# Layer 0 with all seven outer products split into seven unit products, third sums kept in place, and new orders

## The chip, the cores and the metric

The kernel runs on one core of one Trainium2 chip. The metric is the device time of one execution in microseconds (us). TensorE (PE in profiles) multiplies; its weight loads are shown apart as PEld. VectorE is DVE, ScalarE is ACT, GpSimd is POOL, and SyncE (SP) issues nearly all transfers. TensorE's results go to PSUM, eight banks of 512 float32 columns on 128 partitions. GpSimd does not read PSUM in this kernel: VectorE and ScalarE take results out.

## The reference

There are 64 graphs ("batches" b) of 256 nodes with 512 features. Everything is float32.

```python
def layer0(x, adj, W):                       # W: 512 x 1024
    deg = jnp.sum(adj, axis=-1, keepdims=True)
    agg = jnp.einsum('bij,bjf->bif', adj, x) / jnp.maximum(deg, 1e-6)
    out = jnp.einsum('bnf,of->bno', jnp.concatenate([x, agg], axis=2), W)
    return jax.nn.relu(out)
x = layernorm(x + layer0(x, adj, W))

def layer1(x, adj, Wq, Wk, Wv, Wo):          # biases left out here
    q, k, v = heads(x @ Wq.T), heads(x @ Wk.T), heads(x @ Wv.T)   # 8 heads of 64
    s = (q @ k.T) * 64 ** -0.5 * (adj + adj)
    return (softmax(s) @ v) @ Wo.T
x = layernorm(x + layer1(x, adj, ...))
```

## The kernel before, in words

**Layer 0 is reordered.** The kernel first multiplies x by both halves of W (for the node itself, m = 0, and for the neighbours, m = 1), and then multiplies the neighbour half, called y, by adj. The tile `oy[b % 2]` holds both results: index m, token half t (rows 0 to 127 or 128 to 255) and output half n (256 columns each).

**Seven products for eight.** Every large product is cut into 2 x 2 blocks and made of seven products and some sums and differences (the Winograd form of Strassen's method). The left sums are called 1 to 4 (`chain_sums`): S1 = A21 + A22, S2 = S1 - A11, S3 = A11 - A21, S4 = A12 - S2. The products are numbered 1 to 7; product 5 uses S1, 6 uses S2, 7 uses S3, 3 uses S4; 1, 2 and 4 use the blocks themselves. Block A21 stands in sums 1 and 3 only. The results are added as they are taken out of PSUM.

**Two levels in layer 0.** For a pair of batches (b even, and b + 1), the outer product k of layer 0 is a product of a 2 x 2 grid (batch of the pair by chunk of 128 features) with a 2 x 2 grid (chunk by m). `split_product(k)` makes it of seven unit products, each one matmul of 128 x 128 with 128 x 256 (line 546): left sums `Ls{k}1` to `Ls{k}4` on GpSimd (line 567), unit products `L{k}{q}` on TensorE, `Le{k}{q}` to take them out (lines 557 on ScalarE, 559 on VectorE). In the kernel before this is done for k in `SPLIT = (1, 5, 6, 7, 3, 4)`. Product 2 is not split: step `L2` makes two matmuls of 512 columns for each batch (line 598), and `Lj2` adds them to block (1, 0) as it stores block (0, 0) (line 603). `La12` and `La22` are sums of blocks on GpSimd (lines 607, 611). The first pair of batches (0 and 1) does not use these steps but a one-level form, steps `P1` to `P7`.

**Banks.** A PSUM bank is taken anew for each accumulator, eight in rotation. In the split products and in the product with adj, one accumulator `a` takes products 1, 6, 7 and 4, in turn and each added to the last; a second bank (`cb`) holds two accumulators, `c` (products 5 and 3) in columns 0 to 255 and `b` (product 2) in columns 256 to 511. For the product with adj these are the tiles Ya and Ycb, the steps `Y1` to `Y7` on TensorE (line 709), and `Yk*` and `Yj*` on VectorE (line 731), which scale by the degree and add. `Yk5` and `Yj3` read the half that Y5 and Y3 write; `Yj2` reads the half that Y2 writes.

**Layer 1** has steps Q, V and O in the same one-level form (lines 620, 493), scores `Sa` to `Sd` (817), their masking and maxima `ma` to `md` on VectorE (833), exponentials (`e`, `f`) and scaling (`n`) on ScalarE, a transposition through VectorE and through memory (`T`, `Dw`, `Ds`), and contexts `C0a` to `C1b` (934). `Dz*`, `Dx`, `Dadj`, `Drest`, `Dout` are transfers, `xT`, `aT`, `x1T` transpositions on VectorE, `W*` loads and sums of weights.

**The order** is written out by hand-readable lists and nothing else sets it: each engine executes its instructions in the order of the lists. `START` and `END` name steps with batches; `PLAN` is one turn for two batches, with offsets to the turn's even batch, and runs for 28 turns (`range(FIRST_TURN, B // 2 - LAST_TURNS)`, 2 to 29). A turn holds work of several batches at once: layer 0 of later ones beside layer 1 of earlier ones.

Of the kernel before, what the change touches and what calls it, by code (L numbers as in the profile page):

```python
# [10 lines left out]
ALU = mybir.AluOpType  # L11
AX = mybir.AxisListType

P = 128
# [34 lines left out]
    Dsc:0 bS2:2 Yk1:2 Y2:2 xT0:5 L37:2 bS3:2 xT0:4 Y6:2 Q4:1 bS4:2 Yk6:2 Yj2:2 aS4:2 xT1:4 Qj3:1 Y3:2
    Dza:3 Qk4:1 Y7:2 Le37:2 Yj3:2 Q2:1 Yj7:2 AYr0:2 AYb0:2 Y4:2 L34:2 xT1:5 AYp0:2 Le44:2 C1a:0 Yk4:2  # L50
    AYr1:2 bS1:3 C0a:0 AYn0:2 AYb1:2 xS3:4 C0b:0 Qj2:1 AYp1:2 C1b:0 Le34:2 aT:3 c1:0 Sc:1 bS3:3 c0:0
    Ls11:4 Sd:1 AYn1:2 mc:1 aS1:3 aS3:3 Sa:1 Dway:2 xS1:5 Dza:4 Sb:1 md:1 cS3:0 xS1:4 V2:1 ma:1 Ls51:4
    O2:0 cS1:0 Y5:3 mb:1 Y1:3 Ma:1 Ls12:4 O1:0 aS2:3 O5:0 Ok1:0 Mb:1 bS2:3 Yk1:3 Dz1:2 eb:1 L51:4 Ok5:0
    Mc:1 L15:4 Vj2:1 cS2:0 Y6:3 ec:1 Yk5:3 Y2:3 Ls53:4 Yk6:3 O6:0 Dx:3 Ls14:4 fc:1 aS4:3 Y7:3 Ok6:0
    cS4:0 fa:1 L55:4 Oj2:0 L52:4 Yj7:3 Ls52:4 O7:0 bS4:3 Le51:4 Dadj:4 fb:1 xS3:5 L56:4 Y4:3 ea:1 O3:0
    x1T:2 Y3:3 rb:1 rc:1 yS3:2 Yj3:3 nb:1 Q1:2 Yk4:3 yS1:2 Yj2:3 AYr0:3 V5:2 Qk1:2 ra:1 Oj7:0 AYr1:3
    Q5:2 na:1 AYb0:3 Tb:1 O4:0 yS2:2 Le56:4 nc:1 L12:4 AYp0:3 AYb1:3 Dwb:1 Q6:2 Ta:1 Ls54:4 AYn0:3 Md:1
    AYp1:3 Ok4:0 L57:4 Dwa:1 Qk6:2 Oj3:0 V1:2 Tc:1 AYn1:3 L11:4 Q7:2 lb1:0 Vk1:2 Dwc:1 Le11:4 Le55:4
    lb0:0 Qk5:2 Le12:4 V6:2 lp0:0 Le57:4 Qj7:2 L16:4 Vk6:2 L54:4 ed:1 Dsa:1 Q4:2 xS2:5 Le16:4 Ls13:4
    Le15:4 ln0:0 yS4:2 Dsb:1 L17:4 Le54:4 lp1:0 L53:4 Vk5:2 L13:4 L2:4 Le13:4 xS2:4 ln1:0 Ls71:4 fd:1  # L60
    Ls61:4 V3:2 Dway:3 Ls62:4 Ls64:4 rd:1 Dout:0 Q3:2 nd:1 Ls63:4 Vj3:2 Le53:4 Lj2:4 Le52:4 Qk4:2 L2:5
    Le17:4 Qj3:2 Td:1 L14:4 L61:4 Le14:4 Dwd:1 V2:2 Le61:4 Dsc:1 V7:2 L66:4 Vj7:2 Q2:2 Lj2:5 Drest:1
    Le66:4 L67:4 Qj2:2 L65:4 Dsd:1 V4:2 Le65:4 Le67:4 L62:4 Vj2:2 Vk4:2 L63:4 Le62:4 L64:4 deg:4 xS4:5
    Sa:2 aT:4 xS4:4 Sc:2 Le64:4 Dz1:3 bo:1 C0a:1 C1a:1 ma:2 Dzx:7 C0b:1 Ls31:4 Le63:4 c0:1 Ls72:4 mc:2
    C1b:1 Ls32:4 Ma:2 Ls74:4 c1:1 Dx:4 Sb:2 Ls34:4 fa:2 La12:4 Sd:2 mb:2 L75:4 cS1:1 L35:4 md:2 Ls73:4
    L71:4 Mb:2 O1:1 Mc:2 La12:5 ec:2 L32:4 Ok1:1 Dadj:5 O5:1 Le71:4 eb:2 Md:2 x1T:3 L72:4 cS2:1 O2:1
    ed:2 Le75:4 aS1:4 Le72:4 O6:1 Ls33:4 fb:2 Le35:4 cS3:1 L76:4 aS3:4 ea:2 L33:4 Le76:4 cS4:1 L73:4
    Ok6:1 L31:4 Le33:4 fd:2 Le73:4 O7:1 Le31:4 rb:2 fc:2 Ok5:1 L41:4 ra:2 Oj7:1 L77:4 Le32:4 na:2 L36:4
    Ls41:4 Le77:4 O4:1 Le36:4 rd:2 Oj2:1 bS1:4 L74:4 Ok4:1 Y1:4 rc:2 yS1:3 Ta:2 nc:2 O3:1 La22:4 Q5:3
    Le74:4 Dwa:2 Oj3:1 nb:2 Dzx:6 Ls42:4 Le41:4 yS3:3 deg:5 Y5:4 L37:4 bS2:4 nd:2 L45:4 Le37:4 V5:3  # L70
    aS2:4 Tb:2 La22:5 L46:4 L34:4 Tc:2 Dwb:2 Ls44:4 Q1:3 Dsa:2 bS3:4 Le45:4 Ls43:4 Le46:4 Yk1:4 yS2:3
    L42:4 Qk1:3 Le34:4 L47:4 Dwc:2 Y6:4 Le47:4 Vk5:3 V1:3 Td:2 aS4:4 L44:4 Vk1:3 L43:4 Le42:4 Qk5:3
    Dwd:2 Le44:4 V6:3 Dsb:2 Le43:4 Yk5:4 Q6:3 lb1:1 Yk6:4 lb0:1 Y3:4 Dsc:2 Qk6:3 yS4:3 Y7:4 Q2:3 lp1:1
    Yj7:4 Vk6:3 xT0:6 Yj3:4 bS3:5 ln1:1 xT1:6 Y2:4 bS4:4 Q7:3 xT1:7 Dsd:2 lp0:1 V7:3 ln0:1 Qj7:3 Y4:4
    Vj7:3 Dout:1 V3:3 Yk4:4 xT0:7 V2:3 Vj3:3 xS1:7 Yj2:4 Q3:3 AYr0:4 xS1:6 Dza:5 AYb0:4 Q4:3 Qj3:3
    AYr1:4 AYb1:4 V4:3 Qk4:3 Qj2:3 AYp1:4 C1a:2 Drest:2 Dza:6 C0a:2 AYp0:4 AYn1:4 C0b:2 Ls13:6 AYn0:4
    C1b:2 Ls51:6 aT:5 Vk4:3 Dway:4 c0:2 Vj2:3 aS1:5 Sa:3 c1:2 Ls11:6 Sb:3 bS1:5 ma:3 cS1:2 Sc:3 cS3:2
    Sd:3 mb:3 aS3:5 bo:2 O2:2 mc:3 Y1:5 Y5:5 Dx:5 O5:2 Yk1:5 Ma:3 md:3 aS2:5 O1:2 ea:3 Ls52:6 bS2:5 Y2:5
    Dz1:4 fa:3 L15:6 Ok1:2 Mb:3 cS2:2 Y6:5 L51:6 ra:3 Oj2:2 bS4:5 L11:6 Yk6:5 O6:2 Yk5:5 aS4:5 Le11:6
    Le51:6 Md:3 Ls53:6 Y7:5 ed:3 Ok6:2 Mc:3 Y3:5 Yj2:5 Ls12:6 L12:6 cS4:2 Yj3:5 fc:3 L56:6 Ok5:2 L16:6  # L80
    Le56:6 O7:2 AYr0:5 Le16:6 ec:3 O3:2 Yj7:5 Oj7:2 na:3 AYb0:5 Y4:5 L55:6 Yk4:5 L57:6 AYp0:5 Oj3:2 L2:6
    AYr1:5 fd:3 AYb1:5 AYn0:5 O4:2 rc:3 x1T:4 AYp1:5 nc:3 L17:6 L2:7 lb0:2 Ls54:6 yS1:4 AYn1:5 Le12:6
    Tc:3 Ls14:6 Le55:6 L52:6 Dway:5 Le15:6 eb:3 V1:4 Dadj:6 Le57:6 rd:3 L13:6 Ok4:2 fb:3 Le17:6 L54:6
    lb1:2 Q1:4 xS2:6 nd:3 Dwc:3 Le13:6 lp0:2 rb:3 Le52:6 Ta:3 L14:6 Le54:6 xS2:7 Vk1:4 V5:4 Le14:6 Qk1:4
# [70 lines left out]
def kernel(  # L155
# [36 lines left out]
    nc = tc.nc  # L192
# [5 lines left out]
    G = F // 2  # L198
# [70 lines left out]


    OUTER = {1: B11, 2: B21, 3: B22, 4: T4, 5: T1, 6: T2, 7: T3}
    SPLIT = (1, 5, 6, 7, 3, 4)
    w0_inner = const.tile([P, len(SPLIT), 3, G], F32, name="W0_inner")

    def inner_weights(k):
# [756 lines left out]
```

## Time and profile before

| | |
|---|---|
| Median of 3 runs | 3019.8 us (3018.74 to 3021.39) |
| The profiled execution | 3019.61 us, span 3017.7 us |
| TensorE clock granted, mean | 0.997 |
| Busy: TensorE, VectorE, GpSimd, ScalarE | 98%, 74%, 60%, 54% |
| Matmul records | 18700 (two for each float32 matmul) |
| Data moved by DMA | 509.69 MB, 169 GB/s |

A span is the time from the first to the last instruction of the profiled execution. In a timeline each line has the start, the length (both in us), the engine, the source line, the operation, what it writes and reads, the shapes and the number of instructions; a bracket gives the engine's idle time just before and what ended it. In the list of waits a line has who waited for whom, the sum in us, how often, and the longest. In groups of instructions the mean length of one stands behind the busy time. The records of following matmuls overlap, since they are pipelined.

### The profile page before, as it was taken

To read this page: it belongs to the slowest core of one execution; us is meant where nothing else is said; L and a number is where in the kernel's file an instruction comes from. 1 tells how busy PE (TensorE), PEld (TensorE's weight loads), DVE (VectorE), ACT (ScalarE), POOL (GpSimd) and SP (SyncE) were. 2 spreads that over 40 slices of the span, in tenths; PEclk is the share of its full clock that TensorE was granted. 3 is DMA by queue.
4 is the path that set the end of the run, shared out by engine and by line. 5 is a ranking of instruction groups with operands and counts; after the bars stand their busy time and mean duration, and the time that the engine had idled before them with its cause. 6 is when DMAs were issued, how large, how long until landed. Compare 5 with 4: busy or idle time off the path is not lost.

```text
span 3017.7 us, 59666 instructions
## 1 busy us (share of the span) xinstructions
PE 2972.0 (98%) x18700; PEld 2541.1 (84%) x18700; DVE 2219.4 (74%) x6148; ACT 1638.0 (54%) x4999; POOL 1818.5 (60%) x3315
## 2 busy tenths in 40 slices
PE   7999999999999999999999999999999999999997
PEld 4888888888888888888888888888888888888886
DVE  6877777777777777777777877777777777777774
ACT  2556556456555565554554645555556555455465
POOL 5655656656566566566556665666665656656653
PEclk9999999999999999999999999999999999999999
DMA  8476566775666666667656667666676566765663
GB/s 175 130 191 177 147 178 161 185 186 155 174 166 160 193 172 160 174 159 192 177 149 181 157 177 186 166 166 171 156 195 179 147 178 161 186 186 151 178 175 99
DMA packets 491402, 509.69 MB, mean 169 GB/s; under 512 B 113616, under 2 KB 390096, under 8 KB 491088
## 3 DMA queue, kind: packets, MB, share of 16 engines
q1 hardware_dynamic: 490768, 505.35, 64.6%
q8 instruction: 152, 2.49, 0.4%
q14 instruction: 162, 1.33, 0.2%
q10 hardware_dynamic: 320, 0.52, 0.1%
HBM read 306.45 MB, written 199.23 MB: 168 GB/s over the span
## 4 chain that ended last, share of the span: by engine, by line
PE 91%; DMA 3%; DVE 3%; POOL 2%; issue 1%; SPq 0%; ACT 0%; DVEq 0%; ACTq 0%; POOLq 0%
PE Qa L620 15%; PE pc L934 8%; PE Qc L620 8%; PE Va L493 7%; PE Oa L493 6%; PE Qb L620 4%; PE Vc L493 4%; PE L L598 4%; PE Ya L709 3%; PE Oc L493 3%; PE Ycb L709 3%; PE scd L817 2%; DMA z<-way 2%; PE L6a L546 2%; PE L4a L546 2%; PE L3a L546 2%
## 5 line engine op out<-in xcount | busy, mean ns | idle before, releaser
L636 ACT ACTIVATE qk<-Qa,bqk 128x128 f32<-128x128 f32 x768 | 217.9, 366 | 331.7 <-PE Qa L620 331.6
L432 POOL TENSOR_TENSOR xS<-xT,xS 128x256 f32<-128x256 f32 x64 | 47.1, 737 | 286.2 <-PE L6a L546 283.1
L852 ACT ACTIVATE sc<-sc,nmaxc 128x256 f32<-128x256 f32 x256 | 127.0, 498 | 157.7 <-POOL nmaxc L846 147.0
L649 ACT COPY v<-Va 128x256 f32<-128x256 f32 x192 | 73.0, 380 | 240.0 <-PE Va L493 240.0
L950 ACT COPY cT<-pc 128x512 f32<-128x512 f32 x128 | 74.7, 585 | 201.2 <-PE pc L934 197.9
L833 DVE CUSTOM_DVE_ANT_0 sa<-sca,adj 128x256 f32<-128x256 f32 x256 | 93.2, 421 | 110.2 <-PE sca L817 99.4
L852 ACT ACTIVATE sa<-sa,nmaxa 128x256 f32<-128x256 f32 x256 | 127.5, 502 | 68.8 <-DMA z<-way 38.7
L791 POOL TENSOR_TENSOR rest<-rest,bo_sb 128x512 f32<-128x512 f32 x128 | 160.4, 1275 | 0.0
L876 ACT ACTIVATE sc<-sc,totalc 128x256 f32<-128x256 f32 x252 | 107.5, 497 | 96.0 <-DVE totalc L864 96.0
L672 POOL TENSOR_TENSOR mv<-mv,neg_half 128x1 f32<-128x1 f32 x256 | 143.3, 560 | 21.3
L671 POOL TENSOR_SCALAR mv<-mv 128x1 f32<-128x1 f32 x256 | 58.4, 228 | 158.6 <-DVE mv L666 145.0
L731 DVE SCALAR_TENSOR_TENSOR oy<-Ya,deg,oy 128x256 f32<-128x256 f32 x256 | 121.5, 474 | 39.7 <-PE Ya L709 39.5
L833 DVE CUSTOM_DVE_ANT_0 sd<-scd,adj 128x256 f32<-128x256 f32 x256 | 93.1, 420 | 60.5 <-PE scd L817 60.5
L620 PEld LDWEIGHTS Qa<-yS,Wq 128*128 128x128 f32 x1024 | 124.4, 192 | 15.3 <-issue 13.4
L567 POOL TENSOR_TENSOR xs<-xS 128x128 f32<-128x128 f32 x248 | 122.6, 509 | 23.0 <-PE L1a L546 22.8
L677 ACT ACTIVATE x<-oy,mv 128x512 f32<-128x512 f32 x128 | 98.1, 811 | 69.7 <-POOL mv L673 69.7
L611 POOL TENSOR_TENSOR oy<-oy 128x512 f32<-128x512 f32 x62 | 77.9, 1274 | 93.6 <-DVE oy L559 93.4
L876 ACT ACTIVATE sd<-sd,totald 128x256 f32<-128x256 f32 x252 | 107.7, 508 | 45.7 <-DVE totald L864 45.6
L731 DVE SCALAR_TENSOR_TENSOR oy<-Ycb,deg,oy 128x256 f32<-128x256 f32 x192 | 91.4, 477 | 52.9 <-PE Ycb L709 52.7
L852 ACT ACTIVATE sb<-sb,nmaxb 128x256 f32<-128x256 f32 x256 | 126.5, 496 | 6.5 <-POOL nmaxb L846 6.5
L852 ACT ACTIVATE sd<-sd,nmaxd 128x256 f32<-128x256 f32 x256 | 126.7, 497 | 3.4 <-POOL nmaxd L846 3.4
L658 DVE TENSOR_TENSOR rest<-Oa,rest 128x256 f32<-128x256 f32 x192 | 80.3, 418 | 65.2 <-PE Oa L493 42.3
(311 smaller groups left out, 10029.2 us busy)
## 6 DMA issues: line engine op xcount, KB each, us to landing
zx<-in_x_dram SPq DMA_DIRECT2D x256, 128.0 KB, 4.7
x<-in_x_dram SPq DMA_DIRECT2D x256, 128.0 KB, 2.7
way<-x SPq DMA_DIRECT2D x64, 512.0 KB, 3.6
z<-way SPq DMA_DIRECT2D x256, 128.0 KB, 3.9
rest<-way SPq DMA_DIRECT2D x64, 512.0 KB, 4.8
out_dram<-rest SPq DMA_DIRECT2D x256, 128.0 KB, 3.2
wsd<-sd SPq DMA_DIRECT2D x63, 512.0 KB, 4.4
wsb<-sb SPq DMA_DIRECT2D x63, 512.0 KB, 3.8
```

The lines of the kernel that those rows point to most:

```text
L493: nc.tensor.matmul(ps[:, :width].rearrange("p (m o) -> p m o", o=G), lhsT=left(k, b, c), rhs=w(OUTER[k])[:, :, c], start=first and c == 0, ...
L546: nc.tensor.matmul(accumulator(q, b), lhsT=lefts[q](b), rhs=w[q], start=q in (5, 1), stop=True, skip_group_check=True)
L620: nc.tensor.matmul(ps.rearrange("p (m j q) -> p m j q", m=2, j=2)[:, m, j], lhsT=wqk(OUTER[k])[:, m, c, j * P : (j + 1) * P], rhs=left_y(k ...
L636: nc.scalar.activation(part_q(b, t, n)[:, m, j], ps.rearrange("p (m j q) -> p m j q", m=2, j=2)[:, m, j], AF.Identity, bias=bqk[:, m, c : ...
L672: nc.gpsimd.tensor_tensor(mv[:, 1:2], mv[:, 1:2], neg_half, ALU.pow)
L709: nc.tensor.matmul(ps[:, G:] if acc == "b" else ps[:, :G], lhsT=left(b), rhs=right(b), start=k in (5, 1), stop=True, skip_group_check=True,)
L731: nc.vector.scalar_tensor_tensor(h, ps[:, G:] if acc == "b" else ps[:, :G], held["deg", b][:, t : t + 1], h, ALU.mult, ALU.add)
L791: nc.gpsimd.tensor_tensor(rest, rest, bo_sb, ALU.add)
L833: nc.vector.tensor_tensor_reduce(out=s[:, :, :, r], in0=sc(b, j)[:, t].rearrange("p (a c l) -> p a c l", a=A, l=L), in1=held["adj", b][:, ...
L852: nc.scalar.activation(rows(b)[:, r], rows(b)[:, r], AF.Exp, bias=of("nmax", b)[:, r : r + 1], accum_out=of("total", b)[:, r : r + 1],)
L876: nc.scalar.activation(dst, src, AF.Identity, scale=of("total", b)[:, r : r + 1])
L934: nc.tensor.matmul(ps[j * D : (j + 1) * D, hp % 2], lhsT=held["v", b][:, c, h * D : (h + 1) * D], rhs=held[f"s{name}", b][:, :, c, j * NT ...
```

## The change

Product 2 of layer 0 joins the split ones: `SPLIT` becomes `(1, 5, 2, 6, 7, 3, 4)`, the steps `L2` and `Lj2` go, and `L21` to `L27`, `Ls21` to `Ls24`, `Le21` to `Le27` and `W0i2` come. The first results of product 2 (q in 5, 1, 6, 4) are stored with block (1, 0) added, on VectorE. The buffers of small sums alternate over all the products of all pairs. Sums 3 of the left sides `yS` and `cS`, and of y (`bS3`), are written over block A21 (for y, block (0, 1)), which no product reads, in place of a buffer of their own. The three lists are new throughout.

```diff
-    SPLIT = (1, 5, 6, 7, 3, 4)
+    SPLIT = (1, 5, 2, 6, 7, 3, 4)
...
         def place(b, n):
-            return part_of(s, b, [P, 2, 2, P])[:, n]
+            return block(b, 1, 0) if n else part_of(s, b, [P, 2, P])
...
         def unit_sum(b, n):
-            return part_of(f"xs{k}", b, [P, 4, P], tag=f"xs{SPLIT.index(k) % 2}")[:, n - 1]
+            return part_of(f"xs{k}", b, [P, 4, P], tag=f"xs{(b // 2 * len(SPLIT) + SPLIT.index(k)) % 2}")[:, n - 1]
...
-        t, n = {5: (1, 1), 3: (0, 1)}.get(k, (1, 0))
+        t, n = {5: (1, 1), 3: (0, 1), 2: (0, 0)}.get(k, (1, 0))
...
                 if k in (1, 5) and q in (5, 1, 6, 4):
                     nc.scalar.copy(dst, ps)
+                elif k == 2 and q in (5, 1, 6, 4):
+                    nc.vector.tensor_tensor(dst, ps, oy_block(b + beta, m, 1, 0), ALU.add)
                 else:
                     nc.vector.tensor_tensor(dst, ps, dst, ALU.add)
...
-    @step("L2")
-    def _(b):
-        ps = bank("L2", b).rearrange("p (m o) -> p m o", m=2)
-        for c in range(2):
-            nc.tensor.matmul(ps, lhsT=x_block(b, 0, 1)[:, c], rhs=w0(B21)[:, :, c], start=c == 0, stop=c == 1)
-
-    @step("Lj2")
-    def _(b):
-        ps = held["L2", b].rearrange("p (m o) -> p m o", m=2)
-        nc.vector.tensor_tensor(both(b, 0, 0), ps, both(b, 1, 0), ALU.add)
...
     def y_sum(k):
-        return lambda b: part_of(f"yB{int(k == 3)}", b, [P, G])
+        return y_block(0, 1) if k == 3 else lambda b: part_of("yB", b, [P, G])
```

Of the lists, here is the stretch of `PLAN` in which the product with adj of the turn's later batch (+3) stands, before and after, and the stretch after in which product 2 stands:

```diff
-    mc+1 Ls52+4 bo+0 V2+1 mb+1 O2+0 Dx+3 O5+0 ma+1 Mc+1 fc+1 Y5+3 O1+0 aS2+3 Dz1+2 cS2+0 Y1+3 Ok1+0
-    L51+4 Ls12+4 Yk5+3 Y2+3 Yk1+3 Ma+1 Le51+4 bS2+3 O6+0 ec+1 Vj2+1 Oj2+0 Md+1 L56+4 Ok6+0 ed+1 Y6+3
-    Dza+4 L15+4 Yk6+3 aS4+3 O7+0 cS4+0 rc+1 Ok5+0 nc+1 Yj2+3 Y3+3 Mb+1 xS3+4 L55+4 Yj3+3 L52+4 bS4+3
+    Ls51+4 Dz1+2 md+1 Sc+1 Ma+1 bo+0 fa+1 Y5+3 Y1+3 mb+1 ea+1 Dx+3 O2+0 O1+0 aS2+3 Yk1+3 Md+1 ra+1 mc+1
+    O5+0 bS2+3 na+1 Y2+3 cS2+0 L15+4 Dadj+4 Ok1+0 Mb+1 Y6+3 Yk5+3 fd+1 Mc+1 L12+4 cS3+0 Yk6+3 O6+0 ec+1
+    aS4+3 Ls12+4 L11+4 Ls52+4 Ok6+0 Y7+3 Ok5+0 Ls54+4 L51+4 Yj7+3 bS4+3 O7+0 Le51+4 x1T+2 Le11+4 cS4+0
+    fb+1 Y3+3 L56+4 Ls14+4 Yj3+3 Y4+3 ed+1 yS1+2 Oj7+0 L16+4 Yj2+3 O3+0 rd+1 Ta+1 nd+1 O4+0 Yk4+3 V1+2
...
+    Le13+4 V7+2 Le17+4 Dsd+1 L54+4 Qk5+2 Vj7+2 L21+4 xS2+5 L14+4 Le21+4 Ls21+4 aT+4 Le14+4 Q7+2 nb+1
+    yS4+2 xS2+4 L25+4 Ls22+4 Dsc+1 ln1+0 Ls24+4 Tb+1 V3+2 Ls23+4 V4+2 Le25+4 L53+4 Dwb+1 Vk4+2 L26+4
+    Le54+4 Ls61+4 L22+4 Le26+4 aS3+4 L23+4 Ls62+4 lb0+0 L65+4 Dsa+1 Ls63+4 L61+4 lp0+0 L62+4 Le61+4 Q3+2
```

## The prediction

> **What bounds the kernel now.** I read the page first: engine table, then chain.
>
> ```profile
> span 3017.7 us, 59666 instructions
> PE 2972.0 (98%) x18700; PEld 2541.1 (84%) x18700; DVE 2219.4 (74%) x6148; ACT 1638.0 (54%) x4999; POOL 1818.5 (60%) x3315
> ...
> PE 91%; DMA 3%; DVE 3%; POOL 2%; issue 1%; SPq 0%; ACT 0%; DVEq 0%; ACTq 0%; POOLq 0%
> ```
>
> TensorE is the bound: 98% busy and 91% of the chain that ends last; the other engines have a quarter of the span or more to spare. So only TensorE work and TensorE waits move the time. Next, the waits of TensorE:
>
> ```profile
> PE Pa L576 <- DMA zx<-in_x_dram: 10.9, 1, 10.9
> PE Ycb L709 <- DVE oy L731: 8.1, 29, 1.4
> PE Ycb L709 <- POOL nmaxb L846: 4.5, 28, 0.2
> ```
>
> Apart from the start, one tile has repeated waits: Ycb, some 29 and 28 times, so once each per turn of two batches (the list PLAN runs 28 turns). The timeline of TensorE, then of VectorE (L731), shows one turn:
>
> ```profile
> 1524.51 0.59 PE L546 MATMUL L5a<-W_sums,xS 128*128 128x256 f32 x2
> 1525.32 0.70 PE L709 MATMUL Ycb<-oy,aT 128*128 128x256 f32 x2 [0.21 <-DVE oy L731]
> 1525.86 1.03 PE L493 MATMUL Oa<-Wo_sums,cS 128*128 128x256 f32 x4
> 1526.72 0.59 PE L546 MATMUL L5a<-W_inner,xs 128*128 128x256 f32 x2
> 1527.15 0.59 PE L709 MATMUL Ya<-yB,aS 128*128 128x256 f32 x2
> 1527.58 0.59 PE L546 MATMUL L1cb<-W_inner,xs 128*128 128x256 f32 x2
> 1528.01 1.03 PE L493 MATMUL Oa<-Wo,cS 128*128 128x256 f32 x4
> 1529.20 0.67 PE L709 MATMUL Ycb<-oy,aS 128*128 128x256 f32 x2 [0.16 <-POOL nmaxb L846]
> 1529.71 0.59 PE L546 MATMUL L5cb<-W_inner,xs 128*128 128x256 f32 x2
> ```
>
> ```profile
> 1524.79 0.48 DVE L731 SCALAR_TENSOR_TENSOR oy<-Ycb,deg,oy 128x256 f32<-128x256 f32 x1
> ...
> 1528.58 0.47 DVE L731 SCALAR_TENSOR_TENSOR oy<-Ycb,deg,oy 128x256 f32<-128x256 f32 x1
> ```
>
> Read starts, not durations: records overlap (0.59 long, but the next starts 0.43 later). A step of 256 columns has a pitch of 0.43 (1526.72 to 1527.15 to 1527.58 to 1528.01), and a double one 0.86. Two steps break it. Y2 (Ycb<-oy,aT) starts 0.81 after a single step, 0.38 late; the step after Y2 starts 0.54 after it, 0.11 late. Y3 (Ycb<-oy,aS) starts 1.19 after a double step, 0.33 late, and the one after it 0.08 late. Together 0.90 us a turn. Both begin as a VectorE read of the other half of their bank ends: Yk5 reads columns 0 to 255 at 1524.79 and Y2 writes 256 to 511; Yj2 reads the upper half at 1528.58 and Y3 writes the lower. The name nmaxb is a mislabel: its step is long over.
>
> Product 2 of layer 0 on TensorE:
>
> ```profile
> 1545.00 1.88 PE L598 MATMUL L<-W,xT 128*128 128x512 f32 x4
> 1546.71 0.59 PE L546 MATMUL L1a<-W_inner,xT 128*128 128x256 f32 x2
> 1547.15 1.88 PE L598 MATMUL L<-W,xT 128*128 128x512 f32 x4
> 1548.86 1.95 PE L620 MATMUL Qa<-yS,Wq 128*128 128x128 f32 x16
> ```
>
> One batch's L2 takes 1.71 us (two matmuls of 512 columns; a matmul is two records), a pair of batches 3.42.
>
> **What the Trainium skill says.** "PSUM — Partial Sum Buffer", section "PSUM bank collisions raise a hardware error": two engines must not touch one bank at once on the same partitions, even at disjoint columns, and waits are to guard the bank, not the address. The trace agrees: Y2 and Y3 wait for a read of the half that they don't write (0.38 and 0.33 us). "Perfetto Trace Analysis", "Identifying the Most-Contended Engine": a high busy share of matmuls does not tell how near TensorE is to its limit. Agreed: 0.38 us is lost at Y2 and the bracket shows 0.21. The same page, "Matmuls", says that larger matmuls are more efficient where possible. Here not so: 1.71 for two of 512 columns is 0.43 for 256, the pitch of the small ones, so seven small for eight is a real seventh-eighths.
>
> **The change part by part.**
>
> (a) Product 2 as units. The built program has 1519 matmuls of 128x256 at the unit line where it had 1302, and none of 124 of 128x512: 31 pairs, 7 units for 4 long ones. Per pair 7 x 0.43 = 3.01 against 3.42, so -0.41; times 31: **-12.7 us**, wholly on the bounding engine. Only the first pair keeps its old form.
>
> (b) Its evictions: 7 on VectorE of 128x256 (line 559: 0.42 us) replace 2 of 128x512 (line 603: 0.67): +2.9 - 1.3 = +1.6 us per pair. Four more small sums on GpSimd at 0.46 to 0.51 (line 567): +1.9 us per pair. A turn is some 92.6 us, of which VectorE is busy 74%, GpSimd 60%; they become 76% and 62%. Cost 0, hidden under TensorE. Without that cover it is at most 1.6 x 31 = 50 us (VectorE) or 59 (GpSimd). Four weight sums (W0i2) run once on VectorE, 0.57 to 0.85 each by line 287: 2.6 us, in START between V5:0 and Qk1:0, well ahead of L21:2; 0, or +2.6 if bare.
>
> (c) Third sums written over a block that no product reads (yS3, cS3, bS3): as many GpSimd instructions (768 at line 432 before; 640 and 128 after), same sizes, 0. They free SBUF. A new ordering is that S1 must have read the block before S3 overwrites it; both are GpSimd's, in that order already. What they write is freed later than a separate tile was: x1T only when Q7 and V7 are done, but it was held for Q2 and V2 anyway, which come near the end.
>
> (d) The orders. In the old odd half of a turn Y2+3 stood straight behind Yk5+3, Y3+3 straight behind Yj2+3. In the new one Y2+3 stands ahead of Yk5+3 (O2, O1, O5, then Y2, L15, Y6, and only then Yk5), and Y3+3 ahead of both Yj3+3 and Yj2+3. So the two waits change sides: Yk5 now waits on VectorE for Y2. Behind it queue Yk6 and the Ok steps; for Yk5 waits Y3, with L12, O6, L11, Y7, L51, O7 between: 4 x 0.43 + 2 x 0.86 = 3.4 us for a step of 0.48. The even half was clear before and is after. **-0.90 x 28.5 = -25.7 us** (28 turns, and half a turn for what the 29 waits show beyond PLAN).
>
> (e) The rest of the reordering. The closest pairs of product, eviction and next product on one bank in PLAN have 1.3 us of TensorE work between them, in both orders (L51 to L56, for one); the old ones ran without a wait. In the new, Q5+1 takes the place of a bank that Le34 may free with 0.87 us (O3) between, where an eviction of 0.42 and its tail fit narrowly, and Q1 to Q6 has 2.2 us for four ScalarE copies of 0.37 each: tight. Not shown before: I bound (e) by nothing gained, -3 (parts of START), and one wait like Y2's per turn, +0.49 x 28 = +14; I take +1. SP issues as many DMAs (2953 instructions both); weight loads Wv and Wo swap places behind the first four loads, which stay, so the 10.9 us start stays. The seven TensorE gaps that I count in START between 31 and 53 us sum to 6.7 us (1.36, 0.96, 1.13, 0.85, 0.83, 0.93, 0.67) and may grow or shrink by a few; likewise the end, where the last softmax drains. Score and context steps stand together once per batch in both orders, so changes of matmul shape stay.
>
> Sum: the profiled run took 3019.6 us, span 3017.7; it equals the median (3019.8) to 0.2. 3019.6 - 12.7 - 25.7 + 1 = **2982 us**, 1.25% less.
>
> **Rivals.**
> - *Only the units pay.* The waits turn up elsewhere (the tight places of (e)): 3019.6 - 12.7 = 3007, with part of them 2992 to 3007. For: product 2 now holds two banks from L21 to L24, across 14 other TensorE steps, where L2 and Lj2 freed theirs at once. Against: the old order has, away from the halves, no repeated wait at all.
> - *The change misses its wait.* Y2's lateness comes from something else than Yk5, such as its operand; then (d) gives nothing, again near 3007. Against: the read of the other half ends 0.05 us before Y2 starts (1524.79 + 0.48) and 0.15 before Y3 (1528.58 + 0.47), the same way in two places with different operands.
> - *Slower.* Product 2 is a serial chain on VectorE: its first evictions read the result of product 1 and must come before those of product 6 add to the same block. If VectorE is behind there (after its 16 score instructions, which start 0.345 apart, 5.5 us, or a transpose of 1.2), L6 holds TensorE. Price: up to the 2.9 us of seven evictions per turn; from (12.7 + 25.7) / 28.5 = 1.35 us a turn it decides. At 2.0 it gives 3019.6 - 38.4 + 57 = 3038. Against: those 14 other steps lie among the seven, and VectorE idles 26%.
>
> **How the numbers follow.** Measurement resolves about 0.2% (6 us). Forecast 0.71, within 2973 to 2991. Units only, in whole or part, 0.20, 2991 to 3010. About nothing 0.03 (3014 to 3026), slower 0.06. A low end of 2972 takes in (e)'s gain and a START and an end better by some us; a high end of 3003 takes most of the second case. Faster 0.91, same 0.03, slower 0.06.
>
> **What would show it.** Right: TensorE rows at the unit line count 3038, none at 128x512 for layer 0; turns of 91.3 us instead of 92.6; Ycb no longer among TensorE's repeated waits; VectorE waits for Ycb instead. (a) is wrong if unit starts are over 0.45 apart; (d) if Y2 or Y3 still starts late, or another TensorE wait shows some 28 times; the whole if VectorE's L evictions release TensorE waits of over 1 us a turn.

## The result, and the profile after

The changed kernel took 2989.4 us (median of 4 runs, 2988.0 to 2989.9) against 3019.3 us for the kernel before (4 runs beside it, 3018.3 to 3021.4). The ratio is 0.9899 with a 95% interval of 0.9882 to 0.9917: 29.9 us, or 1.0%, faster. The forecast was 2982 us with 2973 to 2991 as its likeliest range, so the direction and the range held. The sum, 37.4 us, was 7.5 us too large. Where these went is the main subject of what follows.

From the page of the kernel after, the engine table and the chain that ended last:

```profile
span 2987.9 us, 60252 instructions
PE 2946.9 (99%) x18886; PEld 2578.8 (86%) x18886; DVE 2255.2 (75%) x6307; ACT 1650.5 (55%) x4999; POOL 1868.5 (63%) x3439
...
PE 96%; DMA 2%; DVE 1%; issue 1%; POOL 1%; ACT 0%; SPq 0%; ACTq 0%; POOLq 0%; DVEq 0%
```

TensorE has 186 records more than before (31 pairs, 14 records in place of 8; these are shorter) and is busy 25 us less. That is more than the shorter records give (12.6, below): part of the old waits stood in the busy time, as at Y2, which was 0.38 late with 0.21 in its bracket. Its share of the chain rose from 91% to 96%: there is less waiting left to remove.

The four longest waits of TensorE after (who waited for whom, us in total, times, longest):

```profile
PE Pa L582 <- DMA zx<-in_x_dram: 10.9, 1, 10.9
PE L2a L550 <- DVE oy L563: 3.3, 1, 3.3
PE p_bv L351 <- DMA Wo<-in_wot_dram: 3.3, 1, 3.3
PE Ya L704 <- POOL yB L573: 2.0, 1, 2.0
```

Ycb's 29 and 28 waits are gone (one of 1.4 us in START is left). Each of these four occurs once, and all lie in the prologue (START). Two are new beside the first kernel, 3.3 us each. In VectorE's list Ycb stands with

```profile
DVE oy L726 <- PE Ycb L704: 8.8, 29, 0.7
```

In the kernel before, VectorE waited for Ycb more, not less (86 times, 52.7 us), so this list alone does not show that a wait changed sides. The timeline does, for one step.

Here is TensorE in the odd half of a turn of the kernel after, and below it two lines of VectorE's:

```profile
1149.39 1.03 PE L497 MATMUL Oc<-Wo_sums,cS 128*128 128x256 f32 x4
1150.25 0.59 PE L704 MATMUL Ycb<-oy,aT 128*128 128x256 f32 x2
1150.68 0.59 PE L550 MATMUL L1cb<-W_inner,xs 128*128 128x256 f32 x2
...
1154.14 1.03 PE L497 MATMUL Oa<-Wo,cT 128*128 128x256 f32 x4
1155.00 0.60 PE L704 MATMUL Ycb<-oy,aS 128*128 128x256 f32 x2
1155.43 0.59 PE L550 MATMUL L5a<-W_inner,xs 128*128 128x256 f32 x2
```

```profile
1150.88 0.48 DVE L726 SCALAR_TENSOR_TENSOR oy<-Ycb,deg,oy 128x256 f32<-128x256 f32 x1 [0.29 <-PE Ycb L704]
...
1155.63 0.48 DVE L726 SCALAR_TENSOR_TENSOR oy<-Ycb,deg,oy 128x256 f32<-128x256 f32 x1
```

Read the starts. Y2 (Ycb<-oy,aT) starts 0.86 after a double step and Y3 (Ycb<-oy,aS) too, and the steps behind both follow after 0.43. Nothing is late. VectorE, at Yk5's read of the other half, now stands idle 0.29 us until Y2 has ended, and nothing on TensorE waits for it.

**The turn.** I measure a turn from the start of V2 of one even batch to that of the next, and take the median of the turns of one profiled run. Before it is 92.58 us, after 91.29: 1.29 less, 36.2 us over 28 turns. The forecast was 91.3.

**The whole span, divided.** Give each TensorE record the start-to-start time that its shape shows where nothing is late (0.216 us for 256 columns; two records make a step of 0.43), add these up, and call all that a record starts later than this a stall. Then the end of TensorE's work is its first start plus the pitches plus the stalls. START stands for stalls ahead of 190 us, the tail for those in the last 30 us of TensorE's work. All from one profiled run each:

| us | pitches | stalls in START | between | tail | TensorE ends |
|---|---|---|---|---|---|
| before | 2912.9 | 17.1 | 57.1 | 10.9 | 3009.1 |
| after | 2900.3 | 26.5 | 31.1 | 9.9 | 2978.9 |
| difference | -12.6 | +9.4 | -26.0 | -1.0 | -30.2 |

The units gave their 12.6, the turns lost 26.0 of waiting, and START took 9.4 back. What is left between START and tail (31.1, some 1.1 a turn) is mostly the changes of matmul shape at scores and contexts, three to a batch at 0.14 to 0.20 us each, which both kernels have.

**START of the kernel after.** Windows of the prologue behind the first transfers, first of before, then of after (the columns behind the length: busy us of PE, PEld, DVE, ACT, POOL; then the granted TensorE clock, the DMA share and GB/s):

```profile
11.00:92.60 81.60, 73.99 (x313) 49.03 (x314) 64.21 (x130) 22.33 (x60) 50.88 (x73) 0.96 0.70 156
```

```profile
11.00:92.60 81.60, 67.49 (x264) 44.04 (x265) 60.74 (x104) 16.63 (x38) 53.13 (x71) 0.92 0.71 154
...
90.00:97.00 7.00, 6.79 (x20) 5.56 (x21) 4.02 (x11) 0.00 (x0) 0.53 (x2) 0.57 0.33 76
```

In the same 81.6 us TensorE executes 264 records in place of 313 (not all of the same shapes). TensorE's timeline shows the first hole, and ScalarE's and SP's the cause:

```profile
54.08 5.84 PE L351 MATMUL p_bv<-Wo,bv_all 128*128 128x256 f32 x16 [3.25 <-DMA Wo<-in_wot_dram]
```

```profile
42.58 0.81 ACT L672 ACTIVATE x<-oy,mv 128x512 f32<-128x512 f32 x1 [0.91 <-POOL mv L668]
43.49 0.39 SPq L759 DMA_DIRECT2D way<-x  x1
44.77 0.39 SPq L325 DMA_DIRECT2D Wo<-in_wot_dram  x1
```

In the new START the load of Wo is queued on SP behind `Dway:0`, the store of the first layer norm's result, which can't be issued before that result is there (ScalarE writes it until 43.39). In the old one Wo was issued at 16.2 us. Step `bv2` (p_bv) needs Wo. The second hole, on TensorE and then VectorE:

```profile
85.86 1.03 PE L497 MATMUL Vc<-Wv,yS 128*128 128x256 f32 x4
90.21 1.22 PE L550 MATMUL L2a<-W,xs 128*128 128x256 f32 x2 [3.32 <-DVE oy L563]
91.22 1.06 PE L550 MATMUL L6a<-W_inner,xs 128*128 128x256 f32 x2
92.08 1.06 PE L550 MATMUL L2cb<-W,xT 128*128 128x256 f32 x2
```

```profile
84.87 0.89 DVE L291 TENSOR_TENSOR W_inner<-W 128x256 f32<-128x256 f32 x1
85.80 1.37 DVE L291 TENSOR_TENSOR W_inner<-W,W_inner 128x256 f32<-128x256 f32 x1
87.09 1.48 DVE L291 TENSOR_TENSOR W<-W 128x256 f32<-128x256 f32 x1
88.49 0.67 DVE L291 TENSOR_TENSOR W_inner<-W,W_inner 128x256 f32<-128x256 f32 x1
89.08 0.41 DVE L565 TENSOR_TENSOR oy<-L6a,oy 128x256 f32<-128x256 f32 x1
89.42 0.41 DVE L563 TENSOR_TENSOR oy<-L2cb,oy 128x256 f32<-128x256 f32 x1
89.75 0.41 DVE L563 TENSOR_TENSOR oy<-L2a,oy 128x256 f32<-128x256 f32 x1
```

L27 writes the accumulator that Le26 (the last line) reads. Le26 stands behind four sets of weight sums, W0i6, W0i3, W0i4 and W0i7, of four instructions each, which in the new START run one soon after the other from 74.5 to 89.2 us. In the old one the same sets start at 78 (W0i6), 102 (W0i3), 57 (W0i4) and 46 us (W0i7). The new set, W0i2, has no part in it. It runs ahead of them, and VectorE is idle for 2.7 us before its next eviction:

```profile
67.00 0.39 DVE L291 TENSOR_TENSOR W_inner<-W 128x256 f32<-128x256 f32 x1
...
68.10 0.42 DVE L291 TENSOR_TENSOR W_inner<-W,W_inner 128x256 f32<-128x256 f32 x1
68.44 1.22 DVE L266 TENSOR_TENSOR Wq<-Wq 128x1024 f32<-128x1024 f32 x1
72.32 0.42 DVE L565 TENSOR_TENSOR oy<-L1a,oy 128x256 f32<-128x256 f32 x1 [2.66 <-ACT oy L561]
```

The hole costs more than its 3.3 us: the steps behind it follow after 0.86 in place of 0.43, and the window above gives a granted clock of 0.57 for 90 to 97 us (in the kernel before it is 1.00 there). These late steps add up to 2.9 us. The Trainium skill, "TensorE: Matmul & The Clock Gate", "What's actually happening", says that the clock falls to half after at least one idle window of some 3.4 us and comes back after at least one such window of work. The trace agrees in kind: a pause of 3.3 us, and then slow steps up to about 96 us.

So the stalls of START are: at L27, 3.5 + 2.9; at p_bv 4.0 for the wait and 2.2 behind it at a clock of 0.50, where the kernel before had 0.4 + 1.3; at V4 (81.81 us), which waits for the eviction Vj7 behind the same weight sums, 1.4. That is +12.3, and the other gaps are 3 us shorter than before: +9.4.

### The profile page after: what moved, and what is told of

It reads as the page before. It is cut to its first block, busy times and chain, and to the rows that moved or that the text cites. A ratio compares the mean times of both kernels' runs of the same rounds, so it can differ in the third digit from the quotient of the medians.

```text
span 2987.9 us, 60252 instructions
## 1 busy us (share of the span) xinstructions
PE 2946.9 (99%) x18886; PEld 2578.8 (86%) x18886; DVE 2255.2 (75%) x6307; ACT 1650.5 (55%) x4999; POOL 1868.5 (63%) x3439
## 4 chain that ended last, share of the span: by engine, by line
PE 96%; DMA 2%; DVE 1%; issue 1%; POOL 1%; ACT 0%; SPq 0%; ACTq 0%; POOLq 0%; DVEq 0%
PE Qa L615 15%; PE pc L929 8%; PE Qc L615 8%; PE Oa L497 7%; PE Va L497 7%; PE Qb L615 4%; PE Oc L497 4%; PE Ya L704 4%; PE Vc L497 4%; PE Ycb L704 3%; PE scc L812 2%; PE sca L812 2%; PE scb L812 2%; PE Vb L497 2%; PE scd L812 2%; PE L6a L550 2%
## 5 line engine op out<-in xcount | busy, mean ns | idle before, releaser
L666 POOL TENSOR_SCALAR mv<-mv 128x1 f32<-128x1 f32 x256 | 68.3, 267 | 369.6 <-DVE mv L661 230.5
L615 PEld LDWEIGHTS Qa<-x1T,Wq 128*128 128x128 f32 x2048 | 248.5, 192 | 6.7 <-issue 0.3
L615 PE MATMUL Qa<-x1T,Wq 128*128 128x128 f32 x2048 | 249.4, 275 | 0.0
L672 ACT ACTIVATE rest<-rest,mv 128x512 f32<-128x512 f32 x128 | 100.8, 809 | 169.7 <-POOL mv L668 169.6
L828 DVE CUSTOM_DVE_ANT_0 sc<-scc,adj 128x256 f32<-128x256 f32 x256 | 92.5, 418 | 113.8 <-PE scc L812 109.3
L847 ACT ACTIVATE sa<-sa,nmaxa 128x256 f32<-128x256 f32 x256 | 127.0, 497 | 54.8 <-POOL nmaxa L841 52.7
L871 ACT ACTIVATE sb<-sb,totalb 128x256 f32<-128x256 f32 x252 | 107.5, 500 | 79.6 <-DVE totalb L859 79.6
L573 POOL TENSOR_TENSOR xs<-xS 128x128 f32<-128x128 f32 x248 | 112.4, 459 | 55.2 <-PE L5cb L550 37.9
L401 DVE STREAM_TRANSPOSE xT<-zx 128x512 f32<-128x512 f32 x128 | 89.3, 700 | 66.8 <-issue 56.1
L497 PE MATMUL Oa<-Wo,cT 128*128 128x256 f32 x512 | 131.7, 380 | 1.1 <-DVE totalb L859 0.6
L497 PE MATMUL Va<-Wv,x1T 128*128 128x256 f32 x512 | 131.5, 379 | 0.0
```

The lines of the kernel that those rows point to most:

```text
L497: nc.tensor.matmul(ps[:, :width].rearrange("p (m o) -> p m o", o=G), lhsT=left(k, b, c), rhs=w(OUTER[k])[:, :, c], start=first and c == 0, ...
L615: nc.tensor.matmul(ps.rearrange("p (m j q) -> p m j q", m=2, j=2)[:, m, j], lhsT=wqk(OUTER[k])[:, m, c, j * P : (j + 1) * P], rhs=left_y(k ...
L672: nc.scalar.activation(dst, src, AF.Identity, bias=mv[:, 0:1], scale=mv[:, 1:2])
L828: nc.vector.tensor_tensor_reduce(out=s[:, :, :, r], in0=sc(b, j)[:, t].rearrange("p (a c l) -> p a c l", a=A, l=L), in1=held["adj", b][:, ...
L847: nc.scalar.activation(rows(b)[:, r], rows(b)[:, r], AF.Exp, bias=of("nmax", b)[:, r : r + 1], accum_out=of("total", b)[:, r : r + 1],)
```

## The experiments

Three theories. **T1:** the turn is right as forecast (units and bank halves), and the missing 7.5 us are the two new holes of START. **T2:** the loss is in the turn: Y2's wait was not for its bank's other half, or the third sums in place or the split product cost something that the other gains cover. **T3:** START's holes cost nothing at the end, since what is late there is waited for anyway.

### The two parts of the turn

**e3_y_order_only**, the kernel before with two pairs of steps exchanged:

```diff
-    L51+4 Ls12+4 Yk5+3 Y2+3 Yk1+3
+    L51+4 Ls12+4 Y2+3 Yk5+3 Yk1+3
...
-    nc+1 Yj2+3 Y3+3 Mb+1
+    nc+1 Y3+3 Yj2+3 Mb+1
```

> The kernel before with two words of PLAN moved and nothing else: Y2+3 stands one place ahead of Yk5+3, and Y3+3 one place ahead of Yj2+3. Product 2 stays whole. Theory 1 (TensorE waited for a read of the other half of its bank): 0.38 + 0.11 + 0.33 + 0.08 us less in each of 28 turns, 24 to 25 us, so about 2994.5, a turn of 91.7 us. Rival A (the wait changes sides: Yk5 now waits for Y2, and Y3 for Yk5, with few steps between): half the gain or less, 3007 or more. Rival B (Y2 was late for its own operand): no gain, 3019.

Measured: 2996.4 us, ratio 0.9925 (0.9912 to 0.9939), turn 91.77: 0.81 less than before. The stalls between START and tail fell from 57.1 to 33.7. Two exchanged pairs in a list of 416 steps take away 23.4 us of stalls, most of what the new kernel gained (the time is some 2 us above the expected 2994.5). Y2 and Y3 start on time in every turn. What is left of the 0.90 is 0.07 us a turn inside the O step ahead of Y3, whose second record starts 0.28 after its first in place of 0.22. Rivals A and B fall.

**e7_own_bank_for_y2**, the kernel before, with its orders, where product 2 of the product with adj has a bank of its own:

```diff
-            name = "Ya" if acc == "a" else "Ycb"
-            ps = bank(name, b) if k in (5, 1) else held[name, b]
+            name = f"Y{acc}"
+            ps = bank(name, b) if k in (5, 1, 2) else held[name, b]
...
-                start=k in (5, 1),
+                start=k in (5, 1, 2),
```

> The kernel before, orders and all, but Y2 writes a bank of its own in place of the upper half of the bank of Y5 and Y3: no two steps share halves of a bank in the product with adj. Theory 1 (the wait is one for the shared bank, not for data or order): Y2 and Y3 start on time, the turn falls to 91.7 us, time to 2994 to 2997, unless the additional bank in the rotation of eight makes new waits, which then show at other steps. Rival A (the wait is for an operand): Y2 and Y3 as late as before, 3018.5. Rival B (banks are the scarce thing: one more in the rotation costs as much as the halves): Y2 on time, but the time between 3000 and 3020.

Measured: 2998.6 us, ratio 0.993 (0.9918 to 0.9943), turn 91.70, 0.88 less than before; the stalls between are 33.6. Order and operands are those of before, and the waits at Y2 and Y3 went. So it was the shared bank, not data and not the place in the order by itself. This version uses three banks where two were used. Its time is 1.6 us above the expected range: it has one new stall of 1.8 us, late in the run, and a tail 2 us longer than before.

**e4_product2_whole**, the kernel after with product 2 not split: `L2` for both batches stands where `L26` stood, then `Lj2` for both, and W0i2 is gone.

```diff
-    SPLIT = (1, 5, 2, 6, 7, 3, 4)
+    SPLIT = (1, 5, 6, 7, 3, 4)
...
-    yS4+2 xS2+4 L25+4 Ls22+4 Dsc+1 ln1+0 Ls24+4 Tb+1 V3+2 Ls23+4 V4+2 Le25+4 L53+4 Dwb+1 Vk4+2 L26+4
+    Tb+1 V3+2 V4+2 L53+4 Dwb+1 Vk4+2 L2+4 L2+5 Lj2+4 Lj2+5 Le54+4 Ls61+4 aS3+4 Ls62+4 lb0+0 L65+4 Dsa+1
```

> The changed kernel with its orders, but product 2 of layer 0 whole again: L2 for both batches and Lj2 for both stand where L26 stood, L21 to L27 with their sums and evictions and W0i2 are left out. Theory 1 (seven units of 0.43 us for four matmuls of 0.855): the turn grows from 91.29 to 91.70 us, 28 turns give +11.5 us; START may gain a few us without W0i2 and the evictions of L2. In all 2993 to 3001. Rival (the units bring nothing, their gain lies in the orders): turn 91.3 us, 2985 to 2989.

Measured: 2999.95 us, ratio 0.9937 (0.9925 to 0.995), turn 91.70. The split is worth 0.41 us a turn, as the sum of (a) had it. Its START has 21.6 us of stalls against 26.5: the wait at L27 is absent, since no unit of product 2 is there to wait. So of the 12.6 us that the units give, START takes 4.9 back in this order. TensorE ends 9.9 apart (the rest is 0.8 between and 1.5 in the tail), and the medians differ by 10.5. W0i2 is gone here too, and it is not missed: the other four sets start at 74.1 instead of 74.5 us, and V4 still waits behind them (1.7 us; 1.2 in the kernel after).

**e8_third_sums_in_place**, the kernel before with yS3, cS3 and bS3 written over the block that no product reads (in half of each turn bS3 stands ahead of bS1 there, so that bS1 reads what bS3 has written and the sums of that batch are not right; the instructions timed are the same).

```diff
-            return part_of(s, b, [P, 2, 2, P])[:, n]
+            return block(b, 1, 0) if n else part_of(s, b, [P, 2, P])
...
-        return lambda b: part_of(f"yB{int(k == 3)}", b, [P, G])
+        return y_block(0, 1) if k == 3 else lambda b: part_of("yB", b, [P, G])
```

> The kernel before with the third sums alone: yS3 and cS3 are written over the block (1, 0) of their left side, bS3 over block (0, 1) of y; orders and product 2 as before. Theory 1 (no time in it, it frees memory): within 1 us of before, 3017.5 to 3019.5. Rival (what is freed later makes a transposition or a copy of the next batch wait): slower by 0.1 us a turn or more, over 3021.

Measured: 3019.5 us, ratio 1.0002 (0.9993 to 1.001), turn 92.58, stalls between 57.1 as before. The new places cost nothing and give nothing by themselves.

T2 falls: each part of the turn is worth what it was taken for.

### START

**e1_wo_early**, the kernel after with the load of Wo issued behind that of Wq:

```diff
-    Yk5:0 Y6:0 Pk4:0 Wq:0 Yk6:0
+    Yk5:0 Y6:0 Pk4:0 Wq:0 Wo:0 Yk6:0
...
-    Pk4:1 Wo:0 xT1:2
+    Pk4:1 xT1:2
```

> The changed kernel with one step moved in START: the load of Wo stands straight behind that of Wq, so ahead of Dzx:3 and of Dway:0, which waits for the first layer norm. Theory 1 (START lost the missing 8 us, and 4 us of it by this late load): the bias product p_bv no longer waits 3.3 us for Wo, and the time falls by 3 to 4 us, to about 2986. Rival (the start is a chain of its own, and the wait only covers the next one, VectorE's weight sums or GpSimd's sums): p_bv starts sooner and TensorE waits as much later, before L1a:2, Va or L2a; under 1 us of gain, 2989.

Measured: 2987.6 us, ratio 0.9898 (0.9884 to 0.9911). Wo is issued at 37.4 us in place of 44.8. The wait at p_bv is gone and START's stalls fell by 4.5, from 26.5 to 22.0; TensorE ends 2.9 sooner. Not all of the 4.5 is Wo's: the wait at L27 is as long as before (3.5), but the slow steps behind it cost 1.8 in place of 2.9. The median is 1.8 lower, which these intervals can't tell from none.

**e2_weight_sums_early**, the kernel after with two of the sets of weight sums moved ahead, behind Wqs2:

```diff
-    bS4:1 Wqs2:0 Ls53:2
+    bS4:1 Wqs2:0 W0i3:0 W0i4:0 Ls53:2
...
-    xS2:3 W0i3:0 Q7:0 Ls63:2 Ls22:2 Ls61:2 Vj7:0 xS3:2 W0i4:0 Drest:0
+    xS2:3 Q7:0 Ls63:2 Ls22:2 Ls61:2 Vj7:0 xS3:2 Drest:0
```

> The changed kernel with two steps moved in START: the inner weight sums W0i3 and W0i4 (four VectorE instructions each, about 2.5 us a step) stand behind Wqs2:0, in the hole in which VectorE waits for the bias product, and not in the crowd of W0i6, W0i3, W0i4, W0i7 between 74 and 90 us. Theory 1 (that crowd holds the evictions of V7, L21 and L26): the waits of Va (1.2), of L2a (3.3) and the six shorter ones behind it (2.9 in sum) mostly go, and the time falls by 4 to 7 us, to 2982 to 2985. Rival (Va and L2a are late for the weights or sums of product 2 themselves): they start as late as before and the time stays at 2989 to 2990.

Measured: 2984.0 us, ratio 0.9883 (0.9869 to 0.9896). The waits at L27 and V4 are gone, START's stalls are 18.8 (7.7 less), TensorE ends 5.3 sooner, and all four runs lie below all four of the kernel after. Part of a gain in START does reach the end, against T3. The wait for Wo stays, 3.9 us.

**e5_both_start_moves**, the moves of e1 and e2 together.

> The changed kernel with both moves in START together: Wo loaded straight behind Wq, W0i3 and W0i4 summed behind Wqs2:0. Theory 1 (two separate losses, one of a transfer, one of a crowd on VectorE): the savings of the single moves add up, 2.9 and 5.3 us of span before, so 7 to 8 us: 2981 to 2982. Rival (one chain: either move takes away the same slack): no better than the second move alone, 2984.

Measured: 2986.7 us, ratio 0.9891 (0.9875 to 0.9906). The two gains don't add: START's stalls are 20.9, some 2 more than with e2's move alone. A new wait stands at the head of TensorE's list behind the first transfer, and VectorE's timeline shows where it comes from:

```profile
PE Ya L704 <- DVE oy L726: 5.3, 1, 5.3
```

```profile
58.87 1.37 DVE L291 TENSOR_TENSOR W_inner<-W,W_inner 128x256 f32<-128x256 f32 x1
60.16 0.41 DVE L291 TENSOR_TENSOR W<-W 128x256 f32<-128x256 f32 x1
...
61.96 0.42 DVE L291 TENSOR_TENSOR W_inner<-W_sums,W_inner 128x256 f32<-128x256 f32 x1
62.30 0.68 DVE L361 TENSOR_TENSOR bo_sb<-p_bv,bo_sb 128x512 f32<-128x512 f32 x1
62.90 0.47 DVE L726 SCALAR_TENSOR_TENSOR oy<-Ya,deg,oy 128x256 f32<-128x256 f32 x1
```

Y4:1 waits for Yj7:1 (the last line), and Yj7:1 stands behind the moved sums. In e2 that stretch of VectorE's queue was a hole: in the kernel after, VectorE sat idle 4.6 us there for p_bv, that is for Wo. With Wo early the hole is gone, and the sums put there are in the way. That T1's two savings would add was wrong.

**e9_wo_early_sums_spread**: Wo behind Wq as in e1; W0i3 stays, and W0i7 and W0i4 move later, each nearer to the product that first uses it.

```diff
-    Q3:0 W0i7:0 Wos4:0
+    Q3:0 Wos4:0
...
-    V2:0 Qj7:0 L62:2
+    V2:0 Qj7:0 W0i7:0 L62:2
...
-    Q6:1 Le77:2 Ls41:2
+    Q6:1 Le77:2 W0i4:0 Ls41:2
```

> The changed kernel with Wo loaded straight behind Wq, and in START W0i7 moved behind Qj7:0 and W0i4 behind Le77:2, to where VectorE has pauses, so that no weight sum stands ahead of the evictions of Y7:1, V7:0 or the first ones of product 2. Theory 2 (VectorE's queue in START is one budget: in the run with both moves the sums stood where no hole was left once Wo came early, and Yj7:1 waited behind them): now both savings show, L2a and Y4:1 wait under 1 us, 2980 to 2982. Rival (the two moves take the same slack): 2984 or more.

Measured: 2983.8 us, ratio 0.988 (0.9866 to 0.9895), START's stalls 18.8. The time lies between what Theory 2 and its rival expected. L27 and p_bv no longer wait; but Y4:1 (Ya) now waits 1.3, where under 1 was expected, and L4a 1.0. In its windows the clock holds (compare 0.57 after the hole above):

```profile
85.00:97.00 12.00, 12.00 (x86) 10.49 (x85) 11.72 (x43) 4.18 (x17) 7.22 (x13) 1.00 0.19 46
```

**e10_sums_spread_only**: e9 without the move of Wo.

> The changed kernel with Wo where it was and only W0i7 and W0i4 moved, as in the run beside it. Theory 2: L2a no longer waits 3.3 us and the short waits behind it go, as with the sums in the hole before bv3: 2983 to 2985, that is 3 us over the run with Wo early. Rival (same slack): equal to the run with Wo early, within 1 us.

Measured: 2985.9 us, ratio 0.9887 (0.9872 to 0.9901), START's stalls 20.4; the wait for Wo is 3.4. Beside the spread sums the early load is worth 1.6 us of stalls and 2.1 of time, where 3 was expected; alone it was worth 4.5 of stalls (e1), or 3.4 without the shorter slow stretch behind L27. Again the two overlap: once Wo comes early, 1.3 at Ya appears.

**e6_start_and_gpsimd** and **e11_spread_and_gpsimd** add to e5 and e9 an exchange on GpSimd, so that bS2 of batch 1, for which Ya waits 2.0 us, comes sooner:

```diff
-    xS1:2 WqS:0 Y2:1 aS2:1 Yk5:1 aS3:1 bS2:1 bS3:1 Y6:1 Wqs1:0 aS4:1
+    WqS:0 Y2:1 aS2:1 Yk5:1 bS2:1 aS3:1 bS3:1 Y6:1 Wqs1:0 aS4:1 xS1:2
```

> As the run with both START moves, and on GpSimd in START bS2:1 stands ahead of aS3:1 and xS1:2 behind aS4:1, so that the sum for Y6:1 does not queue behind a sum that waits for VectorE. Theory 1 (TensorE's 3.0 us wait for yB before Y6:1 is GpSimd's order): the wait falls below 1.5 us and the time by 1.5 to 2.5 us, to about 2979.5. Rival (bS2:1 is slow by itself or waits for Y5:1): no change, 2981 to 2982.

> As the run with Wo early and the sums spread, and bS2:1 ahead of aS3:1, xS1:2 behind aS4:1 on GpSimd. Theory 2 (GpSimd's order costs TensorE 1 to 2 us at Y6:1, when VectorE is not the next thing late): 1 to 2 us less than the run without it, about 2979.5. Rival (Y6:1 gains and Y3:1, p_bv or L1a:2 lose as much): within 0.7 us of it.

Measured: 2986.6 us (0.9877 to 0.9904) and 2983.2 us (0.9861 to 0.9894). The wait for yB fell from 2.0 to 0.8 in both. Another for aS grew from 1.4 to 1.8, and p_bv waits for Wo again (0.9 and 0.6 us), since TensorE is there sooner. START's stalls are 22.4 and 19.1, no less than without the exchange, and the 1 to 2 us expected did not come: the gain at one wait is lost at the next. e6 also had more slow steps than e5 in START (a granted clock of 0.50 in place of 0.75 from 62.2 to 68.9 us).

The divided span of all, in the manner of the table above:

| us | stalls in START | between | tail | TensorE ends |
|---|---|---|---|---|
| e1 Wo early | 22.0 | 31.4 | 11.4 | 2976.1 |
| e2 two sets early | 18.8 | 31.3 | 12.2 | 2973.6 |
| e5 both | 20.9 | 31.4 | 12.4 | 2976.1 |
| e6 both, GpSimd | 22.4 | 31.4 | 10.8 | 2975.9 |
| e9 Wo early, sums spread | 18.8 | 31.3 | 11.4 | 2972.7 |
| e10 sums spread | 20.4 | 31.3 | 10.8 | 2973.7 |
| e11 as e9, GpSimd | 19.1 | 31.3 | 11.3 | 2973.0 |
| e3 two exchanges | 17.4 | 33.7 | 11.0 | 2986.0 |
| e7 own bank | 17.1 | 33.6 | 13.0 | 2987.5 |
| e4 product 2 whole | 21.6 | 31.9 | 11.4 | 2988.8 |
| e8 in place | 16.0 | 57.1 | 11.0 | 3007.9 |

The column "between" hardly moves with START: 31.1 to 31.4 in all with the new turns and units. The tail varies between 9.9 and 13.0 even where its order is the same (e3 and e7), and START itself by some 1 us with the same order (17.1 before, 16.0 in e8). The tail goes with the granted clock in those 30 us. It is 1.00 in the kernel after, which has the shortest tail, 0.94 in the six kernels with tails of 10.8 to 11.3, and 0.83 or 0.89 in the six with 11.4 to 13.0. Here are the kernel after and e7:

```profile
2948.90:2978.90 30.00, 23.34 (x126) 16.40 (x124) 13.04 (x43) 17.18 (x48) 12.43 (x20) 1.00 0.12 36
```

```profile
2957.50:2987.50 30.00, 23.47 (x110) 15.92 (x108) 10.17 (x26) 15.27 (x42) 9.44 (x17) 0.89 0.13 36
```

Why the clock falls there more in one run than in another is not shown, and each kernel has one profile. So a gain of 2 or 3 us in START need not show at the end of one run: of e2's 7.7, the tail took 2.3. The best versions, e2, e9 and e11, lie at 2983 to 2984 us, some 6 us under the changed kernel; their order among themselves is not resolved. T3 falls, and T1 holds in the main: with both holes gone (e9, e11) the time is within 2 us of the forecast 2982, but the savings of the two don't add.

## Why the prediction was right, and where its sum was off

- **(a) units, -12.7.** Right: the unit line has 3038 records, unit starts are 0.43 apart, the pitches fell by 12.6, and e4 gives 0.41 a turn.
- **(b) evictions and small sums, 0.** Right in the turns: VectorE went from 74% to 75%, GpSimd from 60% to 63%, and no wait of TensorE for an eviction repeats. Right for W0i2 in START too: it took 1.6 us, not 2.6 (0.39 to 0.42 a sum), with an idle stretch behind it, and in e4, without it, V4 waits no less.
- **(c) third sums in place, 0.** Right in time: e8. "In that order already" holds for the new lists only; in the old PLAN bS3 stands ahead of bS1 for the odd batch, so the new place needs the new order.
- **(d) bank halves, -25.7.** Right in mechanism (e3, e7) and in size: the stalls between START and tail fell by 26.0. e3 alone brings 23.4. Yk5 does wait for Y2 now, 0.29 us a turn, hidden. But "VectorE waits for Ycb instead" was a poor sign to look for: it waited for Ycb 86 times before and 29 times after.
- **(e) the rest, +1.** This term failed: it measured +8.4, of which START is +9.4 and the tail -1.0. "Weight loads Wv and Wo swap places behind the first four loads, which stay" counted the first four loads and not what stands ahead of Wo in its new place: the store of the first layer norm, for which SP waits (4.5 more at p_bv than before, with the slow steps behind it). And it did not look at the weight sums that the new START moves: four old sets now stand together on VectorE, and whoever stood behind paid, 1.4 at V4 and 6.4 at L27, of which 2.9 are slow steps after the pause (e2 and e9, which move two of the sets, take away the wait at L27). The upper bound of (e), +14, was drawn for a wait in every turn, so that +8.4 lies inside it, and the time inside the likeliest range, is luck. In the turns (e) was right: the tight places at Q5 and Q1 to Q6 produced no repeated wait.
- **The rivals.** "Only the units pay" and "misses its wait" fell with e3 and e7, "slower" with the list of waits: TensorE waits for an eviction of product 2 once in the whole run, at L27 in START. The mechanism of that third rival, VectorE late at product 2, did occur, but only there, and behind weight sums, not behind scores or a transposition.

The sum with the measured terms: -12.6 - 26.0 + 9.4 - 1.0 = -30.2 us; the spans differ by 29.8.

## What to carry to other kernels

Look for pairs in the order lists in which a product follows straight behind a read of the other half of its bank: exchanging two such pairs was worth 22 us of 3019, and only start times showed all of it (the list of waits had 12.6 us). In a prologue, count for each moved step the queue that it enters and all that stands ahead of it there (a load behind a store that waits, an eviction behind four sets of weight sums), since little other work covers it. A hole that one delay makes is no free place: work put into it is in the way as soon as the delay is mended (e5), so savings in a prologue are tried together before they are added.

## What the runs showed of the hardware

- A pause of TensorE of 3.3 us cost 2.9 us more afterwards: steps at 0.86 us in place of 0.43, with a granted clock of 0.50 until 95.9 us. In e1 the same wait at L27, as long, cost 1.8, since the clock was back after some 3.4 us. In e9, without the pause, it is 1.00. So one pause of this length had two prices. The kernel after, then e1:

```profile
90.20:95.90 5.70, 5.69 (x13) 4.56 (x14) 2.72 (x7) 0.00 (x0) 0.00 (x0) 0.50 0.41 93
```

```profile
86.70:90.20 3.50, 3.50 (x9) 2.78 (x10) 2.53 (x6) 0.00 (x0) 0.00 (x0) 0.52 0.30 87
90.30:97.00 6.70, 6.70 (x49) 5.88 (x49) 5.11 (x14) 1.14 (x4) 3.19 (x6) 1.00 0.16 31
```

- The same weight sum of 128x256 on VectorE, with both inputs in SBUF, took 0.38 to 1.49 us. Two windows of e5 side by side, then two of the kernel after (columns as above; the busy time of POOL is the fifth):

```profile
58.17:60.16 1.99, 0.00 (x0) 0.00 (x0) 1.96 (x3) 0.00 (x0) 1.79 (x2) 1.00 0.59 137
60.16:62.30 2.14, 0.00 (x0) 0.00 (x0) 2.10 (x8) 0.00 (x0) 0.00 (x0) 1.00 0.00 0
```

```profile
84.87:88.49 3.62, 2.02 (x11) 1.46 (x9) 3.58 (x4) 0.00 (x0) 3.62 (x4) 1.00 0.06 9
67.00:68.52 1.52, 1.52 (x15) 1.47 (x14) 1.49 (x6) 0.93 (x4) 1.36 (x3) 1.00 0.00 0
```

  In e5, two sums took 0.67 and 1.37 while GpSimd worked, and the six behind them 0.41 to 0.42 while it was idle. The Trainium skill, "GPSIMD Engine Reference", "Specifications", says that VectorE instructions with two SBUF inputs contend with GpSimd for SBUF. The windows agree, and the rivals fall: TensorE is idle in the first window, and transfers are all but absent in the third (a DMA share of 0.06), where three sums took 0.89, 1.37 and 1.48. What GpSimd does counts: in the last window it is busy with instructions of 128x1, and the sums took 0.39 to 0.42. And the 1271 evictions of the split products on VectorE, of the same size but with one input in PSUM, took 0.38 to 0.43, the 610 that GpSimd overlapped almost throughout no longer than the others (median 0.41). For the forecast it means that 0.57 to 0.85 us was not the range of prices for a weight sum.
